# Moments, roots, evictions and sums of the row norm between layers, put in a written VectorE order

## The chip, the cores and the metric

One core of a Trainium2 chip. The metric is the device time of one execution in microseconds (us); three runs of the kernel before are given with their median.

## What is computed

A graph network on 1024 nodes with 512 features and 16384 edges: a graph convolution, four transformer layers, and a second graph convolution. The change lies at the start of layers 1, 2 and 3 (the first layer is 0), in the norm ahead of the attention's queries:

```python
def _ln(x, w, b):
    mu = jnp.mean(x, -1, keepdims=True)
    var = jnp.var(x, -1, keepdims=True)
    return (x - mu) * jax.lax.rsqrt(var + EPS) * w + b
...
for i in range(L):                       # L = 4
    a = _attn(_ln(h, ln2_w[i], ln2_b[i]), cond, Wq[i], Wk[i], Wv[i], Wo[i])
    h = h + a
    u = _ln(h, ln3_w[i], ln3_b[i]) @ geglu_w[i] + geglu_b[i]
    val, gate = jnp.split(u, 2, axis=-1)
    h = h + val * jax.nn.gelu(gate, approximate=False) @ ffo_w[i] + ffo_b[i]
```

`cond` has 16 sequences of 256 rows; keys and values are made from it, the queries from the normalised `h`.

## The kernel before, in words

The 1024 rows of `h` lie in eight blocks of 128 rows. A layer ends with its feed-forward product, in two halves (`ffn_out`): the first finishes the rows of blocks 0, 1, 4 and 5, the second those of 2, 3, 6 and 7. The next layer begins with eight units on TensorE, four of keys and four of values of the first pair of sequences. A unit (`Twelve`) multiplies operands that are split into parts of twelve bits: `begin` multiplies the high and the low parts (`ah`, `al` with `bh`, `bl`: eight matmuls) and lets ScalarE scale the bank in place (L373); `end` adds the product of the mixed parts (`as`, `bs`: four matmuls) and copies the bank out, which ScalarE does for all eight units here (L380). The units are staggered: unit i begins, unit i - 1 ends, and then what `beside[i]` names is done.

```python
for i, u in enumerate(units):
    u.begin()
    if i:
        units[i - 1].end()
    if i in beside:
        beside[i]()
units[-1].end()
```

Beside the units the norm of the rows is made, in five steps for each block of rows:

- moments (`take_moments`, L168 and L169, VectorE), two instructions a block;
- roots (`ready_first`, L151 to L160 and `less` at L1346, VectorE): 12 instructions for four blocks at once, by Newton steps;
- scaling (`scaled_by_act`, L1353, ScalarE): `xn` from `h`, one instruction a block;
- turning (`turn_first`, `turn`): TensorE transposes `xn` into one PSUM bank (L201), and four column groups of it are evicted into `lnT`, by VectorE (L808) or ScalarE (L810), with the norm's weight and bias;
- sums of rows (`sum_first`, L231 to L234): four additions or subtractions for each pair of blocks nb and nb + 4, into `lnS` and in place into `lnT`; `queries` needs them since it multiplies the 2 x 2 blocks of rows and weights with seven products in place of eight.

`queries` (L296) then takes the products in the order `qa` (twice two products, of `lnT` of the blocks 0 to 3), `qb` (of `lnS`), `qc`, `qd`. The scores of the attention follow.

Who evicts in `turn` is set by `by`: before, always `(0, 1)`, so of the four column groups of a bank ScalarE takes the first and third, VectorE the second and fourth.

```python
if by[k % 2]:
    nc.vector.tensor_scalar(to, of, w, b, OP.mult, OP.add)
else:
    nc.scalar.activation(to, of, AF.Identity, bias=b, scale=w)
```

What sets the order: each engine has one queue that runs in order. A scheduler arranges it, but `in_order(engine)` ties the instructions of its block to the order in which they are written. Before, VectorE's instructions of the end of a layer are so tied (the feed-forward additions, the splits of `wk` and `wv`, and at the end the moments and roots of the blocks 2, 3, 6 and 7), and ScalarE's during the eight units. VectorE's evictions and sums during the units are not tied; they come behind the tied stretch. Before, beside unit 1 and 2 ScalarE scales the blocks 0, 1 and 4, 5; beside unit 4 these four blocks are turned, and GpSimd gets the sums of the pairs (0, 4) and (1, 5); beside units 5 and 6 ScalarE scales 2, 3 and 6, 7; beside unit 7 these four are turned. Then VectorE takes the sums of the pairs (2, 6) and (3, 7), and `split_cond` splits the condition of the next pair of sequences (`ah_c` on ScalarE, `al_c` on VectorE at L314, `as_c` on GpSimd at L316). GpSimd also makes sums of the query weights (`wqs`, L238 to L241), behind the split of `wv`.

Of the kernel before, what the change touches and what calls it, by code (L numbers as in the profile page):

```python
# [8 lines left out]
F32 = mybir.dt.float32  # L9
# [8 lines left out]
P = 128  # L18
# [7 lines left out]
def gnn_kernel(  # L26
# [26 lines left out]
    nc = tc.nc  # L53
    pin = tc.keep_in_program_order
# [9 lines left out]
    KC = D // P  # L64
# [13 lines left out]
    small = ctx.enter_context(tc.tile_pool(name="small", bufs=4))  # L78
# [16 lines left out]
    @contextmanager  # L95
    def in_order(engine):

        traced = nc.cur_bb.bb.instructions
        n = len(traced)
        before = next((i for i in reversed(traced) if i.engine == engine), None)  # L100
        yield
        for i in traced[n:]:
            if i.engine == engine:
                if before is not None:
                    tc.add_manual_dep(i, before.name, mybir.DependencyInfo(
                        mybir.DependencyClass.NoSync, mybir.DependencyReason.DATA))
                before = i

    def bank(name):
        return psum.tile([P, 512], F32, tag="bank", name=name)  # L110
# [53 lines left out]
    def moments_into(mv, xts, name):  # L164

        for i, xt in enumerate(xts):
            st = small.tile([P, 6], F32, tag="st", name=f"st_{name}_{i}")
            nc.vector.bn_stats(st, xt)  # L168
            nc.vector.bn_aggr(mv[:, 2 * i:2 * i + 2], st)  # L169
# [48 lines left out]
    LN2W, LN2B, LN3W, LN3B = (i * L * KC for i in range(4))  # L218
# [4 lines left out]
    h = [hall[:, nb, :] for nb in range(NB)]  # L223
# [45 lines left out]
    def save_cond(g):  # L269
        for k in range(2):  # L270
            nc.sync.dma_start(cond_dram[g][:, 1024 * k:1024 * (k + 1)],
                              raw_x[0, g][k].rearrange("p a b -> p (a b)"))
# [65 lines left out]
    def split_cond(l, g):  # L338
        if g < NG:
            if l == 0:  # L340
                save_cond(g)
            conds[g] = left_parts(raw_x.pop((l, g)), f"c_{l}_{g}")
# [39 lines left out]
    def staggered(units, beside):  # L382
# [8 lines that stand above are left out]
# [68 lines left out]
    first = gp.tile([P, 2], F32, name="first")  # L459
# [53 lines left out]
    for nb, xn in enumerate(scaled(xb, mean, root, "x", xb)):  # L513
        with tc.issue_after(cond_turned.ins):
            pt = transposed(xn, f"x{nb}")
        c0 = (nb % 4) * P
# [280 lines left out]
    def acc_tile(name):  # L797
        return accs.tile([P, 512], F32, tag="acc", name=name)

    def turn(xn, to_halves, c0, wcol, bcol, name, by=(0, 1), each=lambda ins: ins):  # L800

        pt = transposed(xn, name, each)
        for k in range(KC):
            to = to_halves[k // 2][:, k % 2, c0:c0 + P]
            of = pt[:, k * P:(k + 1) * P]
            w, b = cols[:, wcol + k:wcol + k + 1], cols[:, bcol + k:bcol + k + 1]
# [4 lines that stand above are left out]
# [166 lines left out]
    class Quad:  # L977
# [12 lines left out]
        def first(self):  # L990
            self.a = bank(f"ga_{self.n}")
            self.product(0, self.a, True)
            self.s1 = acc_tile(f"gs1_{self.n}")
            nc.scalar.copy(self.s1, self.a)
# [319 lines left out]
    def ln_sums(l):  # L1314
        wide = four_wide(f"ln2S_{l}")
        return [wide[:, :2, :], wide[:, 2:, :], slot(f"ln2S_{l}")]

    def sum_first(t, nb):

        c0 = nb % 4 * P  # L1320
        of = [lnT[i][k][:, :, c0:c0 + P] for k in range(2) for i in range(2)]
        return sums_of_b(t, *of, *(x[:, :, c0:c0 + P] for x in lnS))
# [34 lines left out]

    mv_ready, to_scale = {}, []

    def take_moments(l, blocks):  # L1360
        n = len(blocks)
        mv = mv_ready[blocks[0]] = small.tile([P, 2 * n], F32, tag=f"mv{n}", name=f"mv_{l}_{blocks[0]}",
                                              bufs=2)
        moments_into(mv, [h[nb] for nb in blocks], f"ln2_{l}_{blocks[0]}")

    def ready_first(l, blocks):
        mv, name = mv_ready.pop(blocks[0]), f"ln2_{l}_{blocks[0]}"
        to_scale.append(scaled_by_act(blocks, mv, deviations(mv, name), name))

    def turn_first(l, blocks):  # L1370

        for nb in blocks:
            xn, c0 = xns.pop(nb), nb % 4 * P
            turn(xn, lnT[nb // 4], c0, LN2W + l * KC, LN2B + l * KC, f"ln2_{l}_{nb}", each=pin)

    nc.vector.tensor_scalar(cols[:, :2 * L * KC], cols[:, :2 * L * KC], DH ** -0.5, None, OP.mult)
    lnT = [slots_of(2, f"ln2T_0_{i}") for i in range(2)]
# [33 lines left out]
    for l in range(L):  # L1411

        lnS = []
        if l:
            units = keys(l, 0, wk, by=(0, 0)) + values(l, 0, wv, by=(0, 0))
            units[0].to()
            with waiting_for(right_parts.last, mybir.EngineType.Pool):
                wq = weight_sums(wq, f"wqs_{l}")
            to_turn = [0, 1, 4, 5], [2, 3, 6, 7]
        else:  # L1420
            scale_first(1, deviations(mv_first[1], "ln2_0_4"))
            with waiting_for(scale_first.last, mybir.EngineType.Pool):
                wq = weight_sums(wq, "wqs_0")
            kTs[0], vs[0], kTs[1] = (begun[n] for n in ("k0", "v0", "k1"))
            units = keys(0, 0, wk, 2) + values(0, 0, wv, 1)
            to_turn = [0, 1, 2, 3], [4, 5, 6, 7]

        def turn_some():
            nonlocal lnT
            if l:  # L1430
                lnT = [slots_of(2, f"ln2T_{l}_{i}") for i in range(2)]
            turn_first(l, to_turn[0])
            lnS.extend(ln_sums(l))
            if l:
                sum_first(nc.gpsimd, 0)
                sum_first(nc.gpsimd, 1)

        beside = {len(units) - 1: lambda: turn_first(l, to_turn[1])}
        if l:
            first, then = to_scale  # L1440
            to_scale.clear()
            beside.update({1: lambda: first(0, 1), 2: lambda: first(2, 3), 4: turn_some,
                           5: lambda: then(0, 1), 6: lambda: then(2, 3)})
            with in_order(mybir.EngineType.Activation):
                staggered(units, beside)
        else:
            staggered(units, {2: turn_some, **beside})
        if not l:
            sum_first(nc.gpsimd, 0)
            sum_first(nc.gpsimd, 1)  # L1450
            fetch_cond(2)
        sum_first(nc.vector, 2)
        sum_first(nc.vector, 3)
        split_cond(l, 1)
        qT = queries(l, wq)
        wo = load_w(Wo[l], f"wo_{l}")
        if l:
# [64 lines left out]
        for g in range(NG - 1):  # L1522
# [28 lines left out]
            if g % 2:  # L1551
                blocks = pair_sums(l, g - 1, oTs)
# [38 lines left out]
        f, quads = quads_of(l, 0, left, right)  # L1591
# [25 lines left out]
        lnT = None  # L1617
# [76 lines left out]
        for r in range(1, R):  # L1694
            for c in range(KC):
# [18 lines left out]
                if c == 0:  # L1714
                    kept_f, f = f, chunk.f
# [11 lines left out]
        if last:  # L1727
            w_out, base, again, dinv_row = load_last()
            with waiting_for(Gated.last, mybir.EngineType.Pool):
                w_out = out_weights(nc.gpsimd, L, 0, w_out)  # L1730
            ffn_out(l, R - 1, 0, fT, wff, kept)
        else:
            raw_wk = load_w(Wk[l + 1], f"wk_{l + 1}")
            load_cond(l + 1, 0)
            raw_wv = load_w(Wv[l + 1], f"wv_{l + 1}")
            wk = [[], [], []]

            def split_wk(i):
                for part, t in zip(wk, right_parts(raw_wk[i:i + 1], f"wk_{l + 1}_{i}")):
                    part.extend(t)  # L1740

            half = [0, 1, 4, 5], [2, 3, 6, 7]
            with in_order(mybir.EngineType.DVE):
                ffn_out(l, R - 1, 0, fT, wff, kept, pin, (lambda: split_wk(0), lambda: split_wk(1)))
                ffn_out(l, R - 1, 1, fT, wff, kept, pin, (lambda: ready_first(l + 1, half[0]),
                                                          lambda: None,
                                                          lambda: split_cond(l + 1, 0),
                                                          lambda: take_moments(l + 1, half[0])))
                wq = load_w(Wq[l + 1], f"wq_{l + 1}")
                ffb = load_row(ffo_b, (l + 1) * D, f"ffb_{l + 1}")  # L1750
                load_cond(l + 1, 1)
                wv = right_parts(raw_wv, f"wv_{l + 1}")
                take_moments(l + 1, half[1])
                ready_first(l + 1, half[1])


    hs_out = [rows_of("hs_high_out"), rows_of("hs_low_out")]
# [141 lines left out]
```

## Time and profile before

| | |
|---|---|
| median of 3 runs | 2414.62 us (2413.72 to 2414.92) |
| the profiled execution | 2414.67 us |
| its span, first to last instruction | 2412.9 us |
| mean granted TensorE clock | 0.996 |
| TensorE busy | 2360.7 us (98%) |
| VectorE, ScalarE, GpSimd busy | 1571.4, 1000.1, 937.1 us |
| moved by DMA, mean | 57 GB/s |

The profile calls the engines PE (TensorE matmul), PEld (its weight loads), DVE (VectorE), ACT (ScalarE), POOL (GpSimd) and SP (SyncE). A line of a timeline has the start in us from the span's start, the busy time, the engine, the source line, the operation, what it writes and reads (`out<-in`) with shapes, and how many instructions are merged in it; in brackets the idle time ahead of it and what ended that. A line of the windows has the bounds, the length, then for each engine busy time and count (PE, PEld, DVE, ACT, POOL), the granted clock of TensorE as a share of full speed, and the DMA share and rate. A line of the waits has what waited for what, the total in us, how often, and the longest.

### The profile page before, as it was taken

What the parts mean: (1) busy time and instruction counts of PE and PEld (TensorE: products, weight loads), DVE (VectorE), ACT (ScalarE), POOL (GpSimd) and SP (SyncE); (2) the same over time, 40 slices, a digit from 0 to 9 for tenths busy, and PEclk for the clock granted to TensorE, in tenths of its full rate; (3) what the DMA queues carried; (4) which work ended last, traced back from release to release, by engine and by line L of the source; (5) the groups of instructions that cost most, each with busy time, mean ns of one, the idle gap of its engine ahead of it and who ended that gap; (6) DMA issues with size and microseconds to landing.
All of it is one profiled execution on the core that took longest, in us unless ns stands there. A gap on an engine that the chain in (4) does not pass through costs nothing. (4 is left out here: it accounts for less than half of the span.)

```text
span 2412.9 us, 33707 instructions
## 1 busy us (share of the span) xinstructions
PE 2360.7 (98%) x12528; PEld 1773.0 (73%) x12528; DVE 1571.4 (65%) x3016; ACT 1000.1 (41%) x2023; POOL 937.1 (39%) x839
## 2 busy tenths in 40 slices
PE   8999999999989999999999999999998999999999
PEld 5668886677767887577776888477785888667787
DVE  9875446787764445877775444777785444678764
ACT  7445454343344444343244444432334445434320
POOL 0142224575232224564432323555523223456531
PEclk9999999999999999999999999999999999999999
DMA  6142110111301111021202101021121111011140
GB/s 200 28 145 82 60 66 18 48 40 53 109 26 67 40 35 37 22 65 45 95 24 66 63 22 53 9 62 44 44 92 50 48 53 36 18 53 40 49 148 36
DMA packets 108843, 138.31 MB, mean 57 GB/s; under 512 B 8232, under 2 KB 65904, under 8 KB 108672
## 3 DMA queue, kind: packets, MB, share of 16 engines
q1 hardware_dynamic: 106576, 130.64, 16.8%
q0 software_dynamic: 1376, 4.30, 0.5%
q8 instruction: 104, 1.70, 0.3%
q10 hardware_dynamic: 720, 1.11, 0.1%
q14 instruction: 67, 0.55, 0.1%
HBM read 119.25 MB, written 16.78 MB: 56 GB/s over the span
## 5 line engine op out<-in xcount | busy, mean ns | idle before, releaser
L316 POOL TENSOR_TENSOR as_c<-ah_c,al_c 128x512 fp32r<-128x512 f32 x128 | 189.2, 1507 | 208.5 <-DVE al_c L314 202.4
L1122 ACT ACTIVATE g<-g 128x512 f32<-128x512 f32 x192 | 112.1, 584 | 280.0 <-PE g L1108 277.5
L1059 POOL TENSOR_TENSOR gsa<-gha,gla 128x512 fp32r<-128x512 f32 x96 | 125.7, 1331 | 104.1 <-DVE gla L1056 104.1
L373 ACT ACTIVATE v<-v 128x512 f32<-128x512 f32 x127 | 74.0, 582 | 219.5 <-PE v L362 219.5
L362 PE MATMUL v<-bs_wv,as_c 128*128 128x512 f32 x508 | 146.8, 411 | 15.6 <-ACT v L373 15.6
L1059 POOL TENSOR_TENSOR gsb<-ghb,glb 128x512 fp32r<-128x512 f32 x48 | 70.0, 1459 | 218.8 <-DVE glb L1056 218.8
L362 PE MATMUL v<-bh_wv,ah_c 128*128 128x512 f32 x508 | 148.3, 414 | 0.0
L843 ACT ACTIVATE pr<-sc,nmax 128x256 f32<-128x256 f32 x256 | 118.2, 474 | 58.3 <-DVE nmax L838 58.3
L362 PE MATMUL v<-bl_wv,al_c 128*128 128x512 f32 x508 | 138.1, 394 | 0.0
L1108 PE MATMUL g<-gr,gsa 128*128 128x512 f32 x384 | 136.5, 436 | 0.0
L1135 ACT ACTIVATE g<-g,gcols 128x512 f32<-128x512 f32 x96 | 67.5, 703 | 164.8 <-DVE g L1143 161.7
L373 ACT ACTIVATE k<-k 128x512 f32<-128x512 f32 x125 | 72.6, 585 | 150.8 <-PE k L362 150.8
L362 PE MATMUL k<-ah_c,bh_wk 128*128 128x512 f32 x500 | 135.1, 392 | 0.0
L362 PE MATMUL k<-al_c,bl_wk 128*128 128x512 f32 x500 | 134.0, 390 | 0.0
L915 POOL TENSOR_TENSOR os<-oT 128x256 f32<-128x256 f32 x12 | 8.8, 733 | 319.1 <-DVE oT L889 319.1
L362 PE MATMUL k<-as_c,bs_wk 128*128 128x512 f32 x500 | 132.2, 395 | 0.0
L1223 PE MATMUL fa<-wff,fT 128*128 128x256 f32 x512 | 121.9, 381 | 6.7 <-DVE kept L1233 6.7
L362 PEld LDWEIGHTS v<-bs_wv,as_c 128*128 128x128 f32 x508 | 95.7, 192 | 41.5 <-ACT v L373 16.9
L1108 PE MATMUL g<-gr,gha 128*128 128x512 f32 x384 | 122.9, 401 | 0.0
L1108 PE MATMUL g<-gl,gla 128*128 128x512 f32 x384 | 119.0, 391 | 0.0
L1223 PEld LDWEIGHTS fa<-wff,fT 128*128 128x128 f32 x512 | 96.5, 190 | 26.7 <-DVE kept L1233 9.9
L378 DVE COPY kT<-k 128x512 f32<-128x512 f32 x54 | 37.4, 692 | 118.3 <-PE k L362 110.1
(368 smaller groups left out, 5902.6 us busy)
## 6 DMA issues: line engine op xcount, KB each, us to landing
ct<-cond_dram SPq DMA_DIRECT2D x48, 512.0 KB, 4.2
wff<-in_L_gnn_ffo_w_dram SPq DMA_DIRECT2D x32, 512.0 KB, 4.4
gxb<-in_L_gnn_geglu_w_dram SPq DMA_DIRECT2D x96, 128.0 KB, 2.2
gxa<-in_L_gnn_geglu_w_dram SPq DMA_DIRECT2D x96, 128.0 KB, 2.3
cond<-in_L_gnn_cond_dram SPq DMA_DIRECT2D x32, 256.0 KB, 3.7
cond_dram<-ct SPq DMA_DIRECT2D x16, 512.0 KB, 4.0
wk<-in_L_gnn_Wk_dram SPq DMA_DIRECT2D x8, 512.0 KB, 6.2
wv<-in_L_gnn_Wv_dram SPq DMA_DIRECT2D x8, 512.0 KB, 8.3
```

The lines of the kernel that those rows point to most:

```text
L316: nc.gpsimd.tensor_tensor(twelve_bits(s)[:, k, :], h[:, k, :], l[:, k, :], OP.subtract)
L362: pin(nc.tensor.matmul(self.bank, twelve_bits(left[k // 2])[:, k % 2, self.c * P:(self.c + 1) * P], twelve_bits(right[k // 2])[:, k % 2, : ...
L373: nc.scalar.mul(self.bank, self.bank, 1.0 + TINY)
L378: nc.vector.tensor_copy(self.to(), self.bank)
L843: nc.scalar.activation(pr3[:, a, :], ps3[:, a, :], AF.Exp, bias=nmax[:, a:a + 1], accum_out=tot[:, a:a + 1])
L915: t.tensor_tensor(s1, a21, a22, OP.add)
L1059: pin(nc.gpsimd.tensor_tensor(s_at, h_at, l_at, OP.subtract))
L1108: pin(nc.tensor.matmul(to, self.part(i, which)[:, k, :], self.rights[i][which].bitcast(F32R)[:, k, :], start=start and k == 0, stop=stop a ...
L1122: pin(nc.scalar.mul(to, to, 1.0 + TINY))
L1135: pin(nc.scalar.activation(to, of, AF.Gelu, bias=gcols[:, cg:cg + 1]))
L1223: each(nc.tensor.matmul(to[:, q * M:(q + 1) * M], left[i][k][:, (2 * s + q) * P:(2 * s + q + 1) * P], right[i][:, k, :], start=start and q ...
```

## The change

For the layers 1 to 3:

- `turn_first` takes `by` for each block: at unit 4 blocks 0 and 4 are evicted by VectorE alone, 1 and 5 by ScalarE alone; later 2, 3 and 7 by VectorE, 6 by ScalarE.
- The moments and roots of 2, 3, 6 and 7 leave the end of the layer before. At unit 4, in a written VectorE order: moments of 2 and 3, evictions of 0 and 4, moments of 6 and 7, roots, and the sums of the pairs (0, 4) and (1, 5), which GpSimd made before.
- ScalarE scales 2 and 3 beside unit 6 and 6 and 7 beside unit 7, one unit later than before. Blocks 2 and 3 are turned beside unit 7, but 6 and 7 behind the last unit's `end`.
- Behind the units, again in a written VectorE order: the eviction of 7, the sums of (2, 6) and (3, 7), and `al_c` of the next condition; ScalarE's share of it (`ah_c`) is now in ScalarE's written order too.

Layer 0 keeps its order.

```diff
--- before.py
+++ after.py
@@ -1357,21 +1357,24 @@
 
     mv_ready, to_scale = {}, []
 
-    def take_moments(l, blocks):
-        n = len(blocks)
-        mv = mv_ready[blocks[0]] = small.tile([P, 2 * n], F32, tag=f"mv{n}", name=f"mv_{l}_{blocks[0]}",
-                                              bufs=2)
-        moments_into(mv, [h[nb] for nb in blocks], f"ln2_{l}_{blocks[0]}")
+    def take_moments(l, blocks, start=0, stop=None):
+        n, name = len(blocks), f"{l}_{blocks[0]}"
+        stop = stop or n
+        if not start:
+            mv_ready[blocks[0]] = small.tile([P, 2 * n], F32, tag=f"mv{n}", name=f"mv_{name}", bufs=2)
+        moments_into(mv_ready[blocks[0]][:, 2 * start:2 * stop], [h[nb] for nb in blocks[start:stop]],
+                     f"ln2_{name}_{start}")
 
     def ready_first(l, blocks):
         mv, name = mv_ready.pop(blocks[0]), f"ln2_{l}_{blocks[0]}"
         to_scale.append(scaled_by_act(blocks, mv, deviations(mv, name), name))
 
-    def turn_first(l, blocks):
-
-        for nb in blocks:
+    def turn_first(l, blocks, by=((0, 1),)):
+
+        for i, nb in enumerate(blocks):
             xn, c0 = xns.pop(nb), nb % 4 * P
-            turn(xn, lnT[nb // 4], c0, LN2W + l * KC, LN2B + l * KC, f"ln2_{l}_{nb}", each=pin)
+            turn(xn, lnT[nb // 4], c0, LN2W + l * KC, LN2B + l * KC, f"ln2_{l}_{nb}",
+                 by[i % len(by)], pin)
 
     nc.vector.tensor_scalar(cols[:, :2 * L * KC], cols[:, :2 * L * KC], DH ** -0.5, None, OP.mult)
     lnT = [slots_of(2, f"ln2T_0_{i}") for i in range(2)]
@@ -1416,42 +1419,53 @@
             units[0].to()
             with waiting_for(right_parts.last, mybir.EngineType.Pool):
                 wq = weight_sums(wq, f"wqs_{l}")
-            to_turn = [0, 1, 4, 5], [2, 3, 6, 7]
         else:
             scale_first(1, deviations(mv_first[1], "ln2_0_4"))
             with waiting_for(scale_first.last, mybir.EngineType.Pool):
                 wq = weight_sums(wq, "wqs_0")
             kTs[0], vs[0], kTs[1] = (begun[n] for n in ("k0", "v0", "k1"))
             units = keys(0, 0, wk, 2) + values(0, 0, wv, 1)
-            to_turn = [0, 1, 2, 3], [4, 5, 6, 7]
 
         def turn_some():
             nonlocal lnT
             if l:
                 lnT = [slots_of(2, f"ln2T_{l}_{i}") for i in range(2)]
-            turn_first(l, to_turn[0])
-            lnS.extend(ln_sums(l))
-            if l:
-                sum_first(nc.gpsimd, 0)
-                sum_first(nc.gpsimd, 1)
-
-        beside = {len(units) - 1: lambda: turn_first(l, to_turn[1])}
+                with in_order(mybir.EngineType.DVE):
+                    take_moments(l, half[1], 0, 2)
+                    turn_first(l, half[0], ((1, 1), (0, 0)))
+                    take_moments(l, half[1], 2)
+                    ready_first(l, half[1])
+                    lnS.extend(ln_sums(l))
+                    sum_first(nc.vector, 0)
+                    sum_first(nc.vector, 1)
+            else:
+                turn_first(0, range(4))
+                lnS.extend(ln_sums(0))
+
+        def turn_more():
+            to_scale[0](2, 3)
+            with in_order(mybir.EngineType.DVE):
+                turn_first(l, half[1][:2], ((1, 1),))
+
         if l:
-            first, then = to_scale
-            to_scale.clear()
-            beside.update({1: lambda: first(0, 1), 2: lambda: first(2, 3), 4: turn_some,
-                           5: lambda: then(0, 1), 6: lambda: then(2, 3)})
             with in_order(mybir.EngineType.Activation):
-                staggered(units, beside)
+                first = to_scale.pop()
+                staggered(units, {1: lambda: first(0, 1), 2: lambda: first(2, 3), 4: turn_some,
+                                  6: lambda: to_scale[0](0, 1), 7: turn_more})
+                to_scale.clear()
+                with in_order(mybir.EngineType.DVE):
+                    turn_first(l, half[1][2:], ((0, 0), (1, 1)))
+                    sum_first(nc.vector, 2)
+                    sum_first(nc.vector, 3)
+                    split_cond(l, 1)
         else:
-            staggered(units, {2: turn_some, **beside})
-        if not l:
+            staggered(units, {2: turn_some, len(units) - 1: lambda: turn_first(0, range(4, 8))})
             sum_first(nc.gpsimd, 0)
             sum_first(nc.gpsimd, 1)
             fetch_cond(2)
-        sum_first(nc.vector, 2)
-        sum_first(nc.vector, 3)
-        split_cond(l, 1)
+            sum_first(nc.vector, 2)
+            sum_first(nc.vector, 3)
+            split_cond(l, 1)
         qT = queries(l, wq)
         wo = load_w(Wo[l], f"wo_{l}")
         if l:
@@ -1750,8 +1764,6 @@
                 ffb = load_row(ffo_b, (l + 1) * D, f"ffb_{l + 1}")
                 load_cond(l + 1, 1)
                 wv = right_parts(raw_wv, f"wv_{l + 1}")
-                take_moments(l + 1, half[1])
-                ready_first(l + 1, half[1])
 
 
     hs_out = [rows_of("hs_high_out"), rows_of("hs_low_out")]
```

## The prediction

> **What bounds the kernel now.** I read the busy times first, then the waits of TensorE, then TensorE's timeline at the places where those waits lie, and last the three other engines there.
>
> ```profile
> span 2412.9 us, 33707 instructions
> PE 2360.7 (98%) x12528; PEld 1773.0 (73%) x12528; DVE 1571.4 (65%) x3016; ACT 1000.1 (41%) x2023; POOL 937.1 (39%) x839
> ...
> PE v L362 <- ACT v L373: 15.6, 3, 5.2
> PE qb L296 <- DVE ln2S L233: 5.4, 3, 1.8
> ```
>
> TensorE is busy 98% of the span, so time can only come from its 52 us of gaps and from stretches in which it runs slowly. The last two rows (us in total, times, longest) are waits that occur once in each of the three changes of layers: one for ScalarE's scaling of a `v` bank, one for VectorE's sums of rows `lnS`. Behind them TensorE is the bound again, as the window below from 712.30 on shows, so what these waits lose or gain stays.
>
> TensorE at the first change of layers (start, us, what; four matmuls to a row):
>
> ```profile
> 683.92 1.17 PE L362 MATMUL v<-bh_wv,ah_c 128*128 128x512 f32 x4
> 684.93 1.07 PE L362 MATMUL v<-bl_wv,al_c 128*128 128x512 f32 x4
> 685.83 1.07 PE L362 MATMUL v<-bs_wv,as_c 128*128 128x512 f32 x4
> ...
> 687.65 1.07 PE L362 MATMUL v<-bl_wv,al_c 128*128 128x512 f32 x4
> 693.91 2.07 PE L362 MATMUL v<-bs_wv,as_c 128*128 128x512 f32 x4 [5.20 <-ACT v L373]
> ...
> 700.42 1.91 PE L201 MATMUL tr_ln<-ident,xn_ln 128*128 128x128 f32 x16
> 702.09 1.17 PE L362 MATMUL v<-bs_wv,as_c 128*128 128x512 f32 x4
> 703.26 7.22 PE L296 MATMUL qa<-ln2T,wq 128*128 128x512 f32 x16
> 712.29 1.96 PE L296 MATMUL qb<-ln2S,wqs 128*128 128x512 f32 x4 [1.80 <-DVE ln2S L233]
> ...
> 693.90:697.00 3.10, 3.08 (x7) 2.48 (x8) 0.00 (x0) 3.10 (x6) 3.02 (x6) 0.50 0.00 0
> ...
> 712.30:730.00 17.70, 17.70 (x48) 7.79 (x52) 6.79 (x11) 0.79 (x1) 0.00 (x0) 1.00 0.35 119
> ```
>
> The stall costs more than its 5.20 us: behind it the granted clock is 0.50 (the window from 693.90, third number from the end), and the 16 `v` matmuls from 693.91 to 700.42 take 6.51 us. Undisturbed, four start 0.90 us after the four before (684.93 to 685.83). The other two changes of layers look alike, with shorter slow stretches:
>
> ```profile
> 1256.33 2.08 PE L362 MATMUL v<-bs_wv,as_c 128*128 128x512 f32 x4 [5.22 <-ACT v L373]
> ...
> 1261.64 1.91 PE L201 MATMUL tr_ln<-ident,xn_ln 128*128 128x128 f32 x16
> ...
> 1817.54 2.07 PE L362 MATMUL v<-bs_wv,as_c 128*128 128x512 f32 x4 [5.21 <-ACT v L373]
> ...
> 1823.76 1.91 PE L201 MATMUL tr_ln<-ident,xn_ln 128*128 128x128 f32 x16
> ```
>
> Now the engines that it waits for, VectorE, ScalarE and GpSimd in turn:
>
> ```profile
> 681.44 0.69 DVE L168 BATCH_NORM_STATS2 st_ln<-hall 128x6 f32<-128x512 f32 x1
> 682.16 0.18 DVE L169 BATCH_NORM_AGGREGATE mv<-st_ln 128x2 f32<-128x6 f32 x1
> 682.26 0.66 DVE L168 BATCH_NORM_STATS2 st_ln<-hall 128x6 f32<-128x512 f32 x1
> ...
> 684.76 0.81 DVE L151 TENSOR_SCALAR v_ln<-mv 128x4 f32<-128x4 f32 x1
> ...
> 685.81 1.13 DVE L156 SCALAR_TENSOR_TENSOR a_ln<-y_ln,v_ln 128x4 f32<-128x4 f32 x1
> ...
> 688.54 0.16 DVE L1346 SCALAR_TENSOR_TENSOR less_ln<-mv,y_ln 128x4 f32<-128x4 f32 x1
> 688.62 0.41 DVE L808 TENSOR_SCALAR ln2T<-tr_ln,cols 128x128 f32<-128x128 f32 x1
> 689.55 0.76 DVE L808 TENSOR_SCALAR ln2T<-tr_ln,cols 128x128 f32<-128x128 f32 x2 [0.53 <-ACT ln2T L810]
> 690.84 0.76 DVE L808 TENSOR_SCALAR ln2T<-tr_ln,cols 128x128 f32<-128x128 f32 x2 [0.53 <-ACT ln2T L810]
> ...
> 711.39 0.41 DVE L232 TENSOR_TENSOR ln2T<-ln2T,ln2T 128x256 f32<-128x256 f32 x1
> 711.73 0.41 DVE L233 TENSOR_TENSOR ln2S<-ln2T,ln2S 128x256 f32<-128x256 f32 x1
> 712.17 0.42 DVE L234 TENSOR_TENSOR ln2S<-ln2T,ln2S 128x256 f32<-128x256 f32 x1
> ...
> 682.95 0.46 ACT L810 ACTIVATE ln2T<-tr_ln,cols 128x128 f32<-128x128 f32 x1
> 689.06 0.81 ACT L810 ACTIVATE ln2T<-tr_ln,cols 128x128 f32<-128x128 f32 x2 [5.65 <-DVE ln2T L808]
> ...
> 693.27 0.59 ACT L373 ACTIVATE v<-v 128x512 f32<-128x512 f32 x1
> ...
> 694.27 1.52 ACT L1353 ACTIVATE xn_ln<-hall,less_ln,y_ln 128x512 f32<-128x512 f32 x2
> ...
> 685.62 1.30 POOL L241 TENSOR_TENSOR wqs<-wq,wqs 128x512 f32<-128x512 f32 x1
> ...
> 703.85 6.34 POOL L316 TENSOR_TENSOR as_c<-ah_c,al_c 128x512 fp32r<-128x512 f32 x4 [6.21 <-DVE al_c L314]
> ```
>
> The chain is: VectorE takes the moments of rows 2, 3, 6, 7 from 681.44 and their roots until 688.70, and only then reaches its first eviction of a transposed block (688.62). ScalarE had evicted its first column of block 0 at 682.95 and then stood 5.65 us, because each bank is shared and the two engines take turns. Behind that, in ScalarE's written order, is the scaling of `v` bank 1 (693.27), for which TensorE's next matmuls wait until 693.91. The alternation itself is slow too: VectorE stands 0.53 us between pairs.
>
> **The change part by part**, laid out on the first change of layers. I go by the instruction order of the changed kernel on each engine.
>
> *Evictions by one engine each, and roots behind them.* VectorE's queue is now moments of 2 and 3 (0.8 each by the first three rows, so until 683.05), block 0, block 4 (four columns each, 0.35 apart by the 0.76 us pair: 1.4 a block, until 685.85), moments of 6 and 7 (until 687.45), roots. ScalarE takes blocks 1 and 5 with nothing to wait for but the transposes: by its pair of 0.81 and its single 0.46 also 0.35 apart, so 1.4 each from 683.2, until 686.0. Then `v` bank 1 is scaled until 686.6, as soon as its matmuls end (685.83 and little more). TensorE wants it at 687.65 + 0.90 = 688.55. So the stall goes, with the slow clock behind it.
>
> *What is late next: the rows 2, 3, 6, 7.* The roots now start at about 687.5. GpSimd's weight sums end at 686.92, so the two root steps that took 0.81 and 1.13 instead of 0.16 meet nothing. From `less_ln`'s end, 688.70, less 684.76, the chain took 3.94 with these two blocked; without their 1.6 excess it is 2.3, so done at 689.85. ScalarE's scalings of 2 and 3 are moved one unit later, behind its copy of `v` bank 1 (until 690.2), and take 1.5 until 691.6; the scaling of `v` bank 3, queued behind them, follows until 692.1; then the copy of bank 2 and rows 6 and 7, at 693.6 and 694.3. TensorE meanwhile, from 688.55: end of `v` 1, `v` 3 begun, end of `v` 2 (four groups of four, 3.63) until 692.19; transposes of 2 and 3 until 693.0; end of `v` 3 until 694.0 (its scaling was there at 692.1); transpose of 6 at 694.0, of 7 at 694.4. Every need is met, that of 7 by 0.1 only. I price this at 0.2 a change of layers, with ends 0 and 1.5 (all of the pair of scalings late).
>
> *Sums of rows.* GpSimd loses its eight sums, VectorE gains them: six at 0.34 and two at 0.44, 2.9 us, behind the roots: 689.85 to 692.8. Rows 2 and 3 follow there (blocks of 1.4, until 695.6), row 7 until 697.0, sums of 2 and 3 until 699.9. The first query product can start at about 695 and needs the first column of row 3 (694.6): no wait. `qb` needs the last sum after the 16 `qa` matmuls, at about 702: 2 us to spare, so the 1.80 us wait goes as well. GpSimd does nothing from 686.92 until `as_c`, so it isn't in the way.
>
> *The split of the next condition* now stands behind the sums on VectorE: `al_c` from about 700 to 703, and GpSimd's `as_c` ends near 706 or 708, some 5 us behind `qb`'s start instead of before it. TensorE uses it about 25 us behind `qb`, so this cover holds. The DMA queues and SyncE's order don't change.
>
> *One more switch.* Transposes of 6 and 7 stand behind the end of `v` 3, so one more change from a transpose to a 12-bit matmul is paid: 1.01 (683.92 to 684.93) against 0.90, 0.1.
>
> **The sum.** Stalls 15.6 and 5.4. Slow stretches: 16 matmuls should take 3.63; they took 6.51, 5.31 and 6.22, so 2.88 + 1.68 + 2.59 = 7.15. The idle time begins at the modelled end of the last matmul (687.65 + 1.07), though the next could have started 0.16 before that: six stalls, 1.0. Together 29.1. Off it 3 × (0.2 + 0.1) = 0.9. Gain 28.2. The profiled execution took 2414.67 us with its span of 2412.9, and the median of the runs is 2414.62, so both give 2386.4.
>
> The trace's slow stretches are 5 to 6.5 us. The Trainium skill, "TensorE: Matmul & The Clock Gate", section "What's actually happening", has the clock halved after an idle window of about 3.4 us and restored after about 3.4 us of work. By its figure each stall would cost 1.7 us behind it, an estimate of 5.1 in all in place of 7.15, and the forecast would be 2388.5; the measured stretches decide. That the 1.80 us waits show no slow row behind them (`qb` 1.96 us for four, at full clock) agrees with it.
>
> **The rivals.**
>
> *The scalings stay late* (chance 0.11). ScalarE's order puts 2, 3, 6, 7 behind VectorE's roots, and the transposes behind ScalarE. If roots or evictions run 2 to 3 us behind my layout, TensorE waits that long at the transposes of 2 or 6, at full clock: 6 to 9 us of the gain stay away, 2392 to 2395. For it: 0.1 us of slack at row 7. Against: all durations are from rows on the same operands.
>
> *The gain is given back* (0.03): `as_c` or another load comes late for the keys of the next group. Then about 2414. Against it, the 25 us of cover.
>
> *The layout fails at VectorE's evictions* (0.02): if ScalarE and VectorE still took turns, now across the banks, four blocks would take 5.2 us as now (one every 1.29, from the pair at 689.55 to that at 690.84), but from 683.05: `v` bank 1 would be scaled at 688.8, 0.3 late, the roots done at 692.2, and rows 6 and 7 about 2.3 late: some 7 to 8 us in all, about 2394.
>
> *Slower, by blocked roots* (0.02). At 684.76 and 685.81 a root step stood until GpSimd's running instruction was over. The roots now come behind the evictions. Were GpSimd's weight sums late enough to cover all 12 root steps, each would cost up to 1.3 (685.62's row) instead of 0.2: 13 us more, so row 2 scaled near 703.7 instead of 690.9, and TensorE would wait 11.5 us at its transposes, with 2.4 of slow clock behind it, against 9.4 gained: 4.5 us lost each, 2428. It decides from 9.4 us of delay on; four sums of 1.3 are 5.2 us, so the group of `as_c` (6.34) would have to run there as well. The Trainium skill, "SBUF — State Buffer", section "Who interferes with whom", states that lock for VectorE instructions with two SBUF inputs, which the sums moved to VectorE are; in this layout no GpSimd instruction runs beside them.
>
> **How the numbers follow.** Forecast 0.82, the rest as above. The likeliest case runs from 2384 (no new cost, 2385.6, less the 1.2 us between the lowest and the highest run before, 2413.72 and 2414.92) to 2391 (3 × 1.5 of late scalings); the first rival reaches 2395. The range 2384 to 2393 takes in the first and half of the second. A measurement tells about 0.2%, 5 us, from no change. Faster: 0.82 + 0.11 + 0.02 = 0.95; same 0.03; slower 0.02.
>
> **What would show it.** Right: no wait of `v` for ScalarE and none of `qb` for `lnS`; granted clock 1.00 throughout; `qb` some 14.6 us behind the `v` group of 687.65 instead of 24.6; VectorE's evictions in fours without gaps. Wrong: a wait at `tr_ln` or `qa` of over 1 us, root steps of about 1 us, or a new wait for `as_c`.

## The result

| | before | changed |
|---|---|---|
| median of 4 runs | 2414.72 us (2413.72 to 2414.92) | 2385.10 us (2384.74 to 2386.67) |
| ratio, with its 95% interval | | 0.9879 (0.9862 to 0.9897) |
| the profiled execution, its span | 2414.67, 2412.9 us | 2384.85, 2383.1 us |

The change saves 29.6 us. The longest waits of TensorE in the changed kernel (us in total, times, longest):

```profile
PE fa L1223 <- DVE kept L1233: 6.7, 8, 0.8
PE edges L481 <- DVE high L467: 3.9, 1, 3.9
PE fd L1223 <- DVE fs L1199: 3.5, 8, 0.4
PE pc L485 <- DMA prow<-in_L_gnn_bn_b_dram: 3.2, 1, 3.2
```

Both waits of the change of layers, of `v` for ScalarE and of `qb` for `lnS`, are gone, and none has come in their place, in these rows or in the smaller ones behind them. TensorE at the first change of layers, from the group that stood ahead of the old stall:

```profile
688.05 1.07 PE L362 MATMUL v<-bl_wv,al_c 128*128 128x512 f32 x4
688.95 1.07 PE L362 MATMUL v<-bs_wv,as_c 128*128 128x512 f32 x4
...
692.58 1.03 PE L201 MATMUL tr_ln<-ident,xn_ln 128*128 128x128 f32 x8
693.37 1.17 PE L362 MATMUL v<-bs_wv,as_c 128*128 128x512 f32 x4
694.39 1.11 PE L201 MATMUL tr_ln<-ident,xn_ln 128*128 128x128 f32 x8
695.33 7.03 PE L296 MATMUL qa<-ln2T,wq 128*128 128x512 f32 x16
702.20 1.88 PE L296 MATMUL qb<-ln2S,wqs 128*128 128x512 f32 x4
...
689.00:695.00 6.00, 6.00 (x34) 5.01 (x33) 5.55 (x20) 5.29 (x9) 0.00 (x0) 1.00 0.00 0
```

No row has an idle time in brackets, and in the window 689 to 695 the clock is 1.00. I use one measure for all kernels below, since it doesn't depend on what lies ahead: from the start of the `v` group at 688.05 to the start of `qb` at 702.20, **14.15 us**. Before, it was 712.29 - 687.65 = **24.64**. At the two later changes of layers it is 14.15 again (1239.94 to 1254.09, 1791.74 to 1805.89). In the kernel before it was 23.46 and 24.37 there:

```profile
1250.05 1.07 PE L362 MATMUL v<-bl_wv,al_c 128*128 128x512 f32 x4
...
1273.51 1.95 PE L296 MATMUL qb<-ln2S,wqs 128*128 128x512 f32 x4 [1.81 <-DVE ln2S L233]
...
1811.26 1.07 PE L362 MATMUL v<-bl_wv,al_c 128*128 128x512 f32 x4
...
1835.63 1.96 PE L296 MATMUL qb<-ln2S,wqs 128*128 128x512 f32 x4 [1.80 <-DVE ln2S L233]
```

The three differences, 10.49, 9.31 and 10.22, make 30.0 us, the whole of the gain (the spans differ by 29.8). Now VectorE and ScalarE in the changed kernel:

```profile
683.46 2.62 DVE L808 TENSOR_SCALAR ln2T<-tr_ln,cols 128x128 f32<-128x128 f32 x8
...
689.97 0.16 DVE L1346 SCALAR_TENSOR_TENSOR less_ln<-mv,y_ln 128x4 f32<-128x4 f32 x1
...
693.30 3.91 DVE L808 TENSOR_SCALAR ln2T<-tr_ln,cols 128x128 f32<-128x128 f32 x12
...
700.03 0.43 DVE L234 TENSOR_TENSOR ln2S<-ln2T,ln2S 128x256 f32<-128x256 f32 x1
...
683.79 2.90 ACT L810 ACTIVATE ln2T<-tr_ln,cols 128x128 f32<-128x128 f32 x8 [0.35 <-PE tr_ln L201]
686.54 0.64 ACT L373 ACTIVATE v<-v 128x512 f32<-128x512 f32 x1
```

Eight evictions run without a gap in 2.6 us on VectorE and beside them eight in 2.9 us on ScalarE, where before all but the first of the sixteen took turns for 5.2. `v` bank 1 is scaled by 687.2, 1.8 us ahead of its matmuls at 688.95. The last sum is done at 700.46, 1.7 us ahead of `qb`.

### The profile page after: what moved, and what is told of

Its sections match the earlier page's. It is cut to its first block, busy times and chain, and to the rows that moved or that the text cites. A ratio compares the mean times of both kernels' runs of the same rounds, so it can differ in the third digit from the quotient of the medians.

```text
span 2383.1 us, 33689 instructions
## 1 busy us (share of the span) xinstructions
PE 2351.5 (99%) x12528; PEld 1769.3 (74%) x12528; DVE 1571.1 (66%) x3052; ACT 994.5 (42%) x2011; POOL 919.0 (39%) x815
## 3 DMA queue, kind: packets, MB, share of 16 engines
q10 hardware_dynamic: 720, 1.11, 0.1%
```

## The experiments

Two theories stood against each other. A: ScalarE was held up because it shared each transposed bank with VectorE; banks of its own free it. B: the place of the moments and roots in VectorE's queue held everything up. Times are given with the kernel before on the same chip; the measure is that of the first change of layers (before 24.64, changed 14.15).

| kernel | us | before | ratio (95%) | measure |
|---|---|---|---|---|
| after_again | 2384.91 | 2414.65 | 0.9875 (0.9858 to 0.9891) | 702.14 - 687.99 = 14.15 |
| evict_alone | 2387.20 | 2417.12 | 0.9878 (0.9862 to 0.9895) | 704.01 - 689.62 = 14.39 |
| evict_first | 2399.78 | 2415.84 | 0.9929 (0.9912 to 0.9945) | 707.57 - 689.83 = 17.74 |
| roots_early | 2390.18 | 2417.12 | 0.9892 (0.9876 to 0.9909) | 703.50 - 687.97 = 15.53 |
| both_evict | 2399.17 | 2417.12 | 0.9930 (0.9913 to 0.9947) | 706.65 - 688.00 = 18.65 |
| sums_gpsimd | 2395.22 | 2417.12 | 0.9912 (0.9895 to 0.9928) | 705.26 - 688.26 = 17.00 |
| rows_not_later | 2387.39 | 2414.65 | 0.9885 (0.9869 to 0.9902) | 702.82 - 687.74 = 15.08 |
| roots_twice | 2390.68 | 2414.65 | 0.9899 (0.9883 to 0.9916) | 703.71 - 687.67 = 16.04 |
| busy_stall | 2410.46 | 2414.65 | 0.9983 (0.9974 to 0.9993) | 710.38 - 687.66 = 22.72 |

**after_again**: the changed kernel, unedited.

> The changed kernel, unedited, beside the others on the same chip: 29 to 30 us below the kernel before, a ratio of 0.988.

29.7 us below the kernel before.

**evict_alone**: the kernel before, with the evictions alone.

```diff
-    def turn_first(l, blocks):
+    def turn_first(l, blocks, by=((0, 1),)):
...
-            turn(..., f"ln2_{l}_{nb}", each=pin)
+            turn(..., f"ln2_{l}_{nb}", by[i % len(by)], pin)
...
+        whose = ((1, 1), (0, 0)) if l else ((0, 1),)
-            turn_first(l, to_turn[0])
+            turn_first(l, to_turn[0], whose)
-        beside = {len(units) - 1: lambda: turn_first(l, to_turn[1])}
+        beside = {len(units) - 1: lambda: turn_first(l, to_turn[1], whose)}
```

> The kernel before with one part of the change alone: in the layers 1 to 3 each transposed block is evicted by one engine (0, 4, 2, 6 VectorE; 1, 5, 3, 7 ScalarE); moments, roots, sums on GpSimd and the place of the turns stay as before. Theory A: no wait of v for ScalarE and none of qb for the sums, clock 1.00: 2385 to 2388, the whole gain. Theory B: the wait of v stays, 5.2 us three times with its slow clock: 2405 to 2415.

29.9 us below before: theory A, and the whole gain with one of the change's parts. ScalarE, then TensorE:

```profile
685.37 2.90 ACT L810 ACTIVATE ln2T<-tr_ln,cols 128x128 f32<-128x128 f32 x8 [0.35 <-PE tr_ln L201]
688.12 0.64 ACT L373 ACTIVATE v<-v 128x512 f32<-128x512 f32 x1
...
690.74 1.52 ACT L1353 ACTIVATE xn_ln<-hall,less_ln,y_ln 128x512 f32<-128x512 f32 x2 [1.24 <-DVE less_ln L1346]
...
690.53 1.07 PE L362 MATMUL v<-bs_wv,as_c 128*128 128x512 f32 x4
...
704.01 1.88 PE L296 MATMUL qb<-ln2S,wqs 128*128 128x512 f32 x4
```

VectorE still takes moments and roots ahead of its own evictions here, but ScalarE needs nothing of it until `less_ln`, so its scaling of `v` is done at 688.8, in time for 690.53.

**evict_first**: the same for the first four blocks only (the difference to evict_alone).

```diff
-        beside = {len(units) - 1: lambda: turn_first(l, to_turn[1], whose)}
+        beside = {len(units) - 1: lambda: turn_first(l, to_turn[1])}
```

> The kernel before with a smaller part of the change: only the first four blocks (0, 4 VectorE; 1, 5 ScalarE) are evicted by one engine each in the layers 1 to 3; the blocks 2, 3, 6 and 7 still take turns. If the two waits of the kernel before belong to the two groups of four separately: the wait for the scaling of v and its slow clock go (15.6 + 7.2 us), the wait of the sums stays or grows to about 2 us each: 2391 to 2392, ratio 0.9905. If the first four alone set both waits: 2385 to 2387, ratio 0.988.

16.1 us gained, less than expected (23 to 24). The waits belong to the two groups of four separately, as expected: that of `v` is gone, that of the sums is there and has grown:

```profile
PE qb L296 <- DVE ln2S L233: 7.3, 3, 2.4
...
PE qa L296 <- ACT ln2T L810: 2.1, 3, 0.7
...
707.57 3.23 PE L296 MATMUL qb<-ln2S,wqs 128*128 128x512 f32 x4 [2.43 <-DVE ln2S L233]
710.59 2.34 PE L296 MATMUL qc<-ln2T,wq 128*128 128x512 f32 x4
...
709.00:710.50 1.50, 1.50 (x3) 0.56 (x2) 0.00 (x0) 0.00 (x0) 0.00 (x0) 0.50 0.86 262
```

Two things were missing in the price: a wait of 0.7 us at `qa` for block 3, and a slow clock, 0.50, behind a wait of only 2.43 us.

**roots_early**: the changed kernel, with moments and roots of 2, 3, 6 and 7 back at the end of the layer before.

```diff
-                    take_moments(l, half[1], 0, 2)
...
-                    take_moments(l, half[1], 2)
-                    ready_first(l, half[1])
...
-                first = to_scale.pop()
+                first = to_scale.pop(0)
...
                 wv = right_parts(raw_wv, f"wv_{l + 1}")
+                take_moments(l + 1, half[1])
+                ready_first(l + 1, half[1])
```

> The changed kernel, but moments and roots of the blocks 2, 3, 6 and 7 are back at the end of the layer before, ahead of VectorE's evictions; one engine still evicts each block. Theory A: ScalarE evicts its two blocks without VectorE, the stall of 5.2 us stays away, but VectorE is 1.3 us late with block 3 for the first query product: 2389. Theory B: with the roots ahead of the evictions the wait of v for ScalarE comes back, 5.2 us with the slow clock behind it, three times: 2405 to 2410.

3 to 4 us above the changed kernel by the ratios (0.9892 against 0.9879 and 0.9875), 4.1 by three times the measure (15.53 - 14.15). The wait of `v` stays away; the one that comes is the expected one, of block 3 at the first query product (longest 1.1):

```profile
PE qa L296 <- DVE ln2T L808: 3.3, 3, 1.1
...
685.10 0.82 DVE L151 TENSOR_SCALAR v_ln<-mv 128x4 f32<-128x4 f32 x1
...
686.16 1.14 DVE L156 SCALAR_TENSOR_TENSOR a_ln<-y_ln,v_ln 128x4 f32<-128x4 f32 x1
...
694.80 3.91 DVE L808 TENSOR_SCALAR ln2T<-tr_ln,cols 128x128 f32<-128x128 f32 x12
```

At the old place two root steps again stand beside GpSimd's weight sums and take 0.82 and 1.14 us, where the changed kernel needs 0.17 and 0.16. That is the 1.6 us by which VectorE comes later to the blocks 2 and 3 (694.80 - 687.97 against 693.30 - 688.05). In evict_alone the same two steps took 0.80 and 1.14, and VectorE still stood idle for 1.53 us ahead of its evictions of 2 and 6. So moving the roots is needed only in this written order, in which the sums of the first pairs stand on VectorE ahead of the evictions of 2 and 3.

**both_evict**: the changed kernel, with all evictions in turns again.

```diff
-                    turn_first(l, half[0], ((1, 1), (0, 0)))
+                    turn_first(l, half[0])
...
-                turn_first(l, half[1][:2], ((1, 1),))
+                turn_first(l, half[1][:2])
...
-                    turn_first(l, half[1][2:], ((0, 0), (1, 1)))
+                    turn_first(l, half[1][2:])
```

> The changed kernel, but every transposed block of the layers 1 to 3 is again evicted column by column in turns by ScalarE and VectorE; the order of moments, roots and sums stays as changed. Theory A (ScalarE is freed by banks of its own): four blocks take 1.29 us each as before, but start at about 683.5 because the roots are out of the way, so the scaling of v bank 1 is only 0.3 us late; the roots end 2.6 us later and the blocks 2 and 3 take turns too, so TensorE waits about 1 us at the transposes and 2.5 us at the first query product: 3.3 us a change of layers, 2395. Theory B (only the place of the roots matters): 2385 to 2387.

4.5 us lost at the first change of layers, 13.5 in three, where 3.3 and 10 were expected; a loss, as theory A says, and B's 2385 to 2387 is excluded. The waits are at the expected places, that of `qa` smaller than the 2.5 expected, and there is a third at `qb`:

```profile
PE qa L296 <- ACT ln2T L810: 2.9, 3, 1.0
PE qb L296 <- DVE ln2S L233: 2.6, 3, 0.9
PE tr_ln L201 <- ACT xn_ln L1353: 2.5, 3, 0.9
...
689.11 1.21 PE L362 MATMUL v<-bs_wv,as_c 128*128 128x512 f32 x4
```

But this kernel is still 18.0 us faster than the kernel before, and its `v` matmuls start only 0.2 us late (689.11, 1.11 us behind the group that starts at 688.00, for 0.90 undisturbed). So the long stall of the kernel before needed both, the shared banks and the roots ahead of VectorE's evictions: either part of the change alone takes it away, and evict_alone's part gives the rest of the gain as well.

**sums_gpsimd**: the changed kernel, with the sums of the first pairs on GpSimd again.

```diff
-                    sum_first(nc.vector, 0)
-                    sum_first(nc.vector, 1)
+                    sum_first(nc.gpsimd, 0)
+                    sum_first(nc.gpsimd, 1)
```

> The changed kernel, but the sums of the pairs (0, 4) and (1, 5) are again made by GpSimd; they now fall beside VectorE's roots (687.7 to 690.1). If a running GpSimd instruction holds up VectorE's root steps, as at 684.76 and 685.81 before, the 12 steps stretch from 2.3 us to 4 to 8 us, the scalings of the last rows come late and TensorE waits 2 to 6 us at each change of layers: 2392 to 2405. If the engines don't hold each other up, or GpSimd is the one that waits: 2385.

2.85 us lost at the first change of layers and 2.89 at the third, within what the first theory gives. GpSimd's sums hold up the root steps (VectorE, then GpSimd, then TensorE):

```profile
688.95 0.66 DVE L156 SCALAR_TENSOR_TENSOR a_ln<-y_ln,v_ln 128x4 f32<-128x4 f32 x1
...
688.85 0.74 POOL L232 TENSOR_TENSOR ln2T<-ln2T,ln2T 128x256 f32<-128x256 f32 x1
...
694.78 1.36 PE L201 MATMUL tr_ln<-ident,xn_ln 128*128 128x128 f32 x8 [1.82 <-ACT xn_ln L1353]
```

A step of 4 elements a partition takes 0.66 in place of 0.16 and ends with GpSimd's instruction (688.95 + 0.66 = 689.61; 688.85 + 0.74 = 689.59). At the second change of layers 3.96 us are lost (1261.80 - 1243.69 = 18.11), since a slow clock follows a wait of about the same length, 1.84 us:

```profile
1250.23 1.36 PE L201 MATMUL tr_ln<-ident,xn_ln 128*128 128x128 f32 x8 [1.84 <-ACT xn_ln L1353]
1251.41 1.89 PE L362 MATMUL v<-bs_wv,as_c 128*128 128x512 f32 x4
```

**rows_not_later**: the changed kernel, with 6 and 7 turned ahead of the last unit's end.

```diff
-                turn_first(l, half[1][:2], ((1, 1),))
+                turn_first(l, half[1], ((1, 1), (1, 1), (0, 0), (1, 1)))
...
-                    turn_first(l, half[1][2:], ((0, 0), (1, 1)))
```

> The changed kernel, but the blocks 6 and 7 are turned ahead of the last unit's end, as before, not behind it. Theory of the prediction (the scalings of 6 and 7 are the late ones): TensorE waits 0.65 us for row 6 and 0.35 for row 7 and starts the queries 1.0 us later at each change of layers, 3 us in all, ratio 0.989. Rival (there is slack): no difference to the changed kernel, or 0.3 less for the switch saved.

2.5 us above the changed kernel on the same chip, 0.93 a change of layers by the measure; expected were 3 and 1.0.

```profile
PE tr_ln L201 <- ACT xn_ln L1353: 1.5, 3, 0.5
```

**roots_twice**: the changed kernel, with the roots of 2, 3, 6 and 7 worked out twice.

```diff
-        to_scale.append(scaled_by_act(blocks, mv, deviations(mv, name), name))
+        root = deviations(mv, name)
+        if blocks[0]:
+            root = deviations(mv, f"{name}_again")
+        to_scale.append(scaled_by_act(blocks, mv, root, name))
```

> The changed kernel, but the roots of the blocks 2, 3, 6 and 7 are worked out twice in a row: 11 more steps on VectorE at 0.2, 2.2 us, at each change of layers. Theory of the prediction (next to no slack from roots over scalings to row 7): the queries start 1.9 us later each time, 5.8 us in all, ratio 0.990. Rival (a slack of 1 us or more in that chain): 3 us or less in all, ratio below 0.9893.

5.8 us above the changed kernel, 1.89 a change of layers, the number that was expected, but in part through another wait:

```profile
PE tr_ln L201 <- ACT xn_ln L1353: 1.1, 3, 0.4
...
PE qa L296 <- DVE ln2T L808: 0.7, 3, 0.2
```

`less_ln` starts 2.08 us later than in the changed kernel (691.67 - 687.67 against 689.97 - 688.05). Of the 1.79 us by which `qa` then starts later, 0.22 is its own wait and 0.17 the lead that it has over the transposes' modelled end where it needn't wait. So the scalings and transposes alone would have made it 1.4 us later, and the chain from the roots over the scalings to row 7 has about 0.7 us of slack. In sums_gpsimd, where `less_ln` is 3.53 us late and nothing waits at `qa`, 2.85 come through, which is the same slack. The rest of the 1.9 is the wait at `qa`: VectorE's chain, from the roots over the first sums to the eviction of block 3, has only about 0.3.

**busy_stall**: the kernel before, with spare work for TensorE in the stall.

```diff
-    def staggered(units, beside):
+    def staggered(units, beside, busy=None):
...
+            if i == busy:
+                spare = bank(f"spare_{u.name}")
+                for n in range(22):
+                    pin(nc.tensor.matmul(spare, twelve_bits(u.left[0][0])[:, 0, :P],
+                                         twelve_bits(u.right[0][0])[:, 0, :],
+                                         start=n == 0, stop=n == 21, skip_group_check=True))
             if i:
                 units[i - 1].end()
...
-                staggered(units, beside)
+                staggered(units, beside, 6)
```

> The kernel before, but TensorE does 22 spare matmuls (128x512, twelve bits, 5 us at full clock) into a bank of their own where it waits for the scaling of v bank 1 in the layers 1 to 3; their result is not used. Theory of the slow clock (the 16 matmuls behind the stall are slow only since TensorE stood idle): granted clock 1.00 there, and 7.15 us less than the kernel before, 2407.5 on its scale of 2414.7; the wait of 1.80 us for the sums grows a little, since VectorE isn't faster, up to all of it: then 2414. Rival (the slow stretch comes from something else, such as ScalarE and VectorE at work): clock still about 0.5 and the time of before.

The clock stays at 1.00 and the sixteen `v` matmuls take 3.76 us (693.96 to 697.72) in place of 6.51, so idleness made the clock slow:

```profile
693.96 1.20 PE L362 MATMUL v<-bs_wv,as_c 128*128 128x512 f32 x4 [0.24 <-ACT v L373]
...
697.72 1.91 PE L201 MATMUL tr_ln<-ident,xn_ln 128*128 128x128 f32 x16
...
701.30 7.22 PE L296 MATMUL qa<-ln2T,wq 128*128 128x512 f32 x16 [0.74 <-ACT ln2T L816]
...
694.00:698.00 4.00, 4.00 (x19) 3.30 (x20) 0.00 (x0) 4.00 (x7) 3.65 (x6) 1.00 0.00 0
```

The time falls by only 4.2 us, not by 7.15: TensorE comes sooner to `qa` and waits there 0.74 us for the evictions in turns (2.2 in three). With ScalarE and VectorE as late as they were, part of the slow clock was hidden behind them.

## Why the prediction was right

- **What bounds it.** Right: the two waits are gone with the slow clock, and the gain of the three changes of layers is the gain of the run.
- **Evictions by one engine each.** The step that carries the gain, and evict_alone shows that it is enough for all of it. The prediction gave it together with "and roots behind them"; for the stall that second half wasn't needed. Nor was the first half: both_evict, which has the rest of the change, gains 18.0 us with `v` 0.2 us late, as the rival *the layout fails* has it (0.3). What the prediction didn't see is that the first half alone is enough. Its layout holds to some tenths of a us: `v` bank 1 scaled by 686.6 in the prediction, 687.2 less the 0.40 by which the changed kernel comes later to this place (688.05 against 687.65), so 686.8.
- **What is late next.** Right in kind and size: `less_ln` ended at 690.13, 689.73 on that scale, for a forecast of 689.85. The price of 0.2 for row 7 wasn't paid: the chain to it has about 0.7 us of slack by roots_twice and sums_gpsimd, for the 0.1 of the prediction. The tightest need is that of `qa` for block 3, with about 0.3, where the prediction had 0.4 (694.6 for 695) and no price.
- **Sums of rows.** Right that they belong behind the roots on VectorE: on GpSimd at this place they cost 2.85 us or more at each change of layers. The eight took 3.25 (690.05 to 693.30), not 2.9: of the steps from one start to the next, four and not two are 0.45 or more. The slack at `qa` and at `qb` covered it.
- **The split of the next condition.** GpSimd's `as_c` ran from 701.67 to 707.5, and TensorE first read it at 726.9, 24.7 us behind `qb`'s start, without a wait.
- **The sum.** 28.2 forecast, 29.6 measured, 30.0 by the three differences. Of the 1.8 between the last and the forecast, 0.6 is the wait of row 7 that wasn't paid; the 16 `qa` matmuls take 7.03 in place of 7.22, which is another 0.6 in three. The last 0.6 is *one more switch*, priced at a loss of 0.1 and measured as a gain of 0.1: the transposes in two parts take 1.73 in place of 1.67 (0.79 from 692.58 and 0.94 from 694.39, against 700.42 to 702.09), but from the last `v` group to what follows it are 1.02 in place of 1.17 (693.37 to 694.39, against 702.09 to 703.26). The 7.15 for the slow clock counted in full because the late evictions that hide part of it in busy_stall went too.
- **The clock by the Trainium skill.** The stretches of this trace were the better price (2386.4, against 2388.5 by the figure of the Trainium skill, "TensorE: Matmul & The Clock Gate", section "What's actually happening"), and evict_first shows that the halving doesn't need the 3.4 us of idleness stated there: 2.43 were enough. In sums_gpsimd 1.84 were, so the 1.80 us waits with the full clock behind them, which the prediction took as agreeing, lend that figure little support. The second change of layers lost 1.68 us to the slow clock, as that figure has it; the first and the third lost 2.88 and 2.59, since there the clock was down for 6.83 us and not for 3.41 (last section).
- **The rivals.** *The layout fails* was priced at 2394; both_evict, which makes the engines take turns in that layout, loses 13.5 us, so some 2399. The prediction priced only the first four blocks; the blocks 2, 3, 6 and 7 take turns too, which is where the waits at `qa` and `qb` come from. *Slower, by blocked roots*: the mechanism is real, sums_gpsimd shows it, but eight sums of 0.7 us make the roots 3.5 us late and cost 2.85 to 3.96, far from the 9.4 at which it would have decided.

## What to carry to other kernels

Where two engines share the eviction of one PSUM bank and take turns, each inherits every delay of the other's queue: here ScalarE stood 5.65 us for the roots on VectorE. Give each engine whole banks, and their queues come apart. Before a long reordering is written, try that alone: here it gave the whole gain, while the rest of the change without it gave 18.0 us. A stall of TensorE costs more than its length when the clock falls behind it, so look at the granted clock in the stretch after each wait; here one of 1.84 us was enough.

## What the runs showed of the hardware that was not expected

In evict_first a wait of 2.43 us was followed by a granted clock of 0.50 at two of the three changes of layers, and one of 2.41 us by none. In sums_gpsimd one of 1.84 us was followed by it, those of 1.82 and 1.86 us weren't, and neither were the waits of 1.80 us in the kernel before. So the length of a wait alone doesn't decide whether the next matmuls run slowly.

The traces show more. In windows of 0.1 us, each slow stretch behind a wait lasts 3.41 us or twice that: in the kernel before from 693.02 to 699.84, from 1256.22 to 1259.63 and from 1816.00 to 1822.83. Their starts are 563.20 and 559.79 us apart, which is 165.0 and 164.0 steps of 3.413 us; the three starts in evict_first (86.88, 708.10 and 1820.84) are 182.0 and 326.0 such steps apart. So within a trace the slow stretches lie on one grid. Cut along it, how long TensorE was busy in one step (the first number behind the length, of 3.41) goes with the clock of the step that follows (evict_first, then sums_gpsimd, then the kernel before):

```profile
704.69:708.10 3.41, 0.98 (x4) 0.33 (x3) 3.12 (x7) 0.59 (x1) 1.32 (x1) 1.00 0.22 10
708.10:711.51 3.41, 3.41 (x6) 1.34 (x5) 0.67 (x1) 0.00 (x0) 0.00 (x0) 0.50 0.74 246
...
1261.06:1264.47 3.41, 2.08 (x5) 0.57 (x3) 3.41 (x5) 1.68 (x4) 2.93 (x3) 1.00 0.25 97
1264.47:1267.88 3.41, 2.34 (x6) 1.17 (x7) 1.66 (x5) 0.00 (x0) 0.00 (x0) 1.00 0.41 154
...
1248.24:1251.65 3.41, 1.52 (x10) 1.08 (x10) 1.64 (x7) 2.29 (x4) 0.40 (x1) 1.00 0.00 0
1251.65:1255.06 3.41, 3.41 (x13) 2.92 (x13) 1.93 (x8) 3.10 (x7) 0.00 (x0) 0.50 0.00 0
...
710.08:713.50 3.42, 1.62 (x4) 0.68 (x4) 2.48 (x7) 0.79 (x2) 0.12 (x1) 1.00 0.22 84
```

The wait of 2.43 us lies within one step, and the clock falls at its end. That of 2.41 us lies across the end of a step, 1.33 and 1.07 us of idleness in the two, and the clock stays. Within one step 1.89 us were enough in sums_gpsimd, and 1.80 us weren't in the kernel before (the clock from 712.30 on was 1.00). Near that the reckoning isn't sharp: at the start of the program 1.97 us in one step of evict_alone (82.53 to 85.94) had the slow clock behind them, and 1.98 us in one of after_again (82.22 to 85.63, counted back from its slow step at the end, 2382.81) the full one. That the clock is decided at the ends of these steps is read from the pattern; no run here shifted one wait along the grid.
